# Layer 0 of a four-layer network: inner channels in three parts of 64, with the two token halves side by side on the partitions

## The chip, the cores and the metric

The kernel runs on one core of a Trainium2 chip, in one launch. The metric is the device time of the whole launch in microseconds, the median of several runs. The core has five engines that work side by side, each through its own instructions in order: TensorE (PE, matrix products into PSUM), VectorE (DVE), ScalarE (ACT), GpSimd (POOL) and SyncE (SP), whose queue issues the DMA transfers here. They wait for each other on semaphores.

## The reference

Four layers follow one another. Only the first is changed; the others (a 7x7 depthwise convolution with an MLP, linear attention with a quantised MLP, a Fourier mixer with a quantised MLP) stay as they are.

Layer 0 takes `x` of shape (4, 96, 64, 64) and reads it as 4 sequences of 4096 tokens with 96 channels. Two Mamba blocks follow, each with 192 inner channels and 16 states per inner channel:

```python
h = layernorm(seq) * ln_g + ln_b
xs, z = split(h @ in_w)                      # 192 inner channels each
xc = silu(causal_conv4(xs) + conv_b)
dt, Bm, Cm = split(xc @ xproj_w)             # 6, 16, 16
delta = softplus(dt @ dt_w + dt_b)
h[t] = exp(delta * A) * h[t-1] + delta * Bm * xc      # 192 x 16 recurrences
y = sum over states of h * Cm  +  Dp * xc
seq = seq + (y * silu(z)) @ out_w
```

A pooled projection, a 1x1 fusion, a batch normalisation over all tokens and the residual close the layer. All of it is float32, except for the products that spread B over the partitions (bfloat16, in three parts that together keep the precision).

## The kernel before, in words

**Items.** The 4096 tokens are cut into 4 chunks of 1024. One item is one chunk of one sequence in one Mamba block: 4 x 2 x 4 = 32 items, in an order that lets the carried states of a sequence (`state`) be ready.

**Tiles.** The recurrences of an item are 192 x 16 = 3072 rows of 1024 tokens, so 24 tiles of 128 rows. A tile's rows are 4 states times 32 inner channels. Its name is (half, g, j): which half of 96 inner channels, which four states, which 32 channels of the half. For each tile

- ACT makes the decay `da` as exp(delta * A) from `ddb`, delta repeated over the four states (`exp`, L472);
- DVE multiplies `udb` (delta * xc, repeated) with `rep`, the rows of B spread over the partitions by a matmul into PSUM (`rep`, `scan`, L488); for 8 of the 24 tiles, the pool tiles, POOL makes this product from `brep`, a copy of B by DMA (`times_b`, L478), and ACT writes the decay, `dap`, into PSUM;
- DVE runs the scan (L492);
- POOL multiplies the result with C, repeated (`times_c`, L498, `crep`);
- PE adds up the states with the matrix `sel_r`, 128 rows to 32 (`sum_y`, L515).

`start_y` begins the sum with Dp * xc, `gate` (L526) multiplies it with z on DVE, `project` (L533, L536) adds the output projection to the residual, and `finish` stores it; in the second block it also takes the statistics of the batch normalisation on DVE (L548).

**PSUM.** The tag `xu` has two buffers of [128, 1024]. They go round between `rep`, the product `u` and `dap`. So a `dap` can only be written when DVE has read the last `rep` before it, and a new `rep` only when the scan of the last tile before the pool tile is done.

**First stage.** The work that prepares an item (layer norm, convolution with four taps, `xproj`, `delta`, `z`, the DMA writes of delta and delta * xc to DRAM, and the loads that bring them back repeated) belongs to `first_stage`. It is spread over slots, one per tile of the item before. SiLU and softplus are ACT functions that need a table load before and one after, back to the exponential's tables.

**Order.** For PE, DVE, ACT and POOL the order of instructions is the order in which the program is written (`manual_schedule`): one iteration per tile m issues the scan of m, the `dap` or `rep` of m + 1, the `da` of m + 3, `times_c` of m - 1, `keep_state` of m - 3, a `times_b` by the table `b_slots`, the sums and gates by their place in the item, and last what `first_stage` keeps for this slot. SP's DMA issues follow the same order, and one that waits holds up those behind it.

Before the change the inner channels lie in two halves of 96 partitions, [96, 2, 1024]. The convolution is four units (half, token half) of four taps each. A half has 12 tiles, and its `y` is [96, 1024] in PSUM, in one buffer of two banks. The order of a half's tiles and the pool tiles among them are

```python
half = [(0, 0), (0, 1), (0, 2), (3, 0), (1, 0), (1, 1), (1, 2), (3, 1), (2, 0), (2, 1), (3, 2), (2, 2)]
pool_tiles = (3, 7, 10, 11)
```

Of the kernel before, what the change touches and what calls it, by code (L numbers as in the profile page):

```python
# [32 lines left out]
for _name, _w in (  # L33
    [(f"{k}{i}", w) for i in range(2) for k, w in (("ln_g", 1), ("ln_b", 1), ("conv_w", 8), ("conv_b", 2), ("Dp", 2))]
# [10 lines left out]
for _name, _w in [("A", 48), ("c_b1", 3), ("f2_b1", 3), ("f3_b1", 3), ("id", 48), ("rd", 48), ("rb", 48), ("ib", 48)]:  # L45
    V128[_name] = (_n, _w)
    _n += _w
# [3 lines left out]
class Net:  # L51
# [41 lines left out]
    def layer0(self, dram, scratch):  # L93
        tc, nc, ins = self.tc, self.nc, self.ins
        x_in = ins["x"]
        with ExitStack() as ctx:
# [3 lines left out]
            psum_y = ctx.enter_context(tc.tile_pool(name="l0y", bufs=1, space=PSUM))  # L100
# [12 lines left out]
            w_x = cp.tile([C + 1, 2, 2, 4, C], F32, name="w_x")  # L113
            w_z = cp.tile([C + 1, 2, 2, C], F32, name="w_z")
            sel_b = cp.tile([C, 4, 128], BF16, name="sel_bq")
            part = cp.tile([C, 2, C], BF16, name="partq")
            fo = cp.tile([C, 2, C], F32, name="fo")
            dp = cp.tile([C, 2, 2, C], F32, name="dp")
            sel_r = load(cp, "sel_r", [128, 32])
            xproj = load(cp, "xproj", [C, 2, 2, 3 * 2 * NST + DTR])  # L120
# [3 lines left out]
            out_w = load(cp, "out_w", [C, 2, 2, C])  # L124
# [6 lines left out]
            with tc.tile_pool(name="l0s", bufs=1) as wk:  # L131
# [17 lines left out]
                for i in range(2):  # L149
# [6 lines left out]
                    for k in range(4):  # L156
                        nc.vector.tensor_mul(
                            w_x[:, i, :, k, :],
                            ps[:, :DIN].rearrange("p (h c) -> p h c", h=2),
                            rows[:, i, k].rearrange("p (h c) -> p h c", h=2),  # L160
                        )
                    b = bias[C:, i].rearrange("p (h c) -> p h c", h=2)
                    nc.vector.tensor_add(w_x[C:, i, :, 3, :], w_x[C:, i, :, 3, :], b)
                    nc.vector.tensor_copy(w_z[:, i], ps[:, DIN:].rearrange("p (h c) -> p h c", h=2))
                    for h in range(2):
                        nc.vector.tensor_scalar_mul(dp[:, i, h, :], self.ident[:C, :C], self.v(f"Dp{i}", h))
# [3 lines left out]
                owt = load(wk, "out_wt", [C, DIN])  # L170
                for h in range(2):
                    ps = small(C, C)
                    nc.tensor.matmul(ps, owt[:, h * C : (h + 1) * C], fus[:, 0, :], start=True, stop=True)
                    nc.vector.tensor_copy(fo[:, h, :], ps)
# [273 lines left out]
            def on_pool(m):  # L448
                return m % 12 in pool_tiles
# [992 lines left out]
```

## Time and profile before

| | |
|---|---|
| median of 3 runs | 4220.64 us (4213.79 to 4222.18) |
| the profiled execution | 4226.66 us, its span 4224.9 us |
| mean granted TensorE clock | 0.893 |
| first scan of layer 0 starts | 84.76 us |
| last scan of layer 0 ends | 2714.65 us |
| busy from 200 to 2600 us: PE, DVE, ACT, POOL | 1974, 2301, 1664, 2302 us of 2400 |
| DMA share and rate in that stretch | 0.56, 150 GB/s |

How to read it. The page's second part cuts the span into 40 slices of 105.6 us and gives each engine's busy share in tenths. A line of a group gives the source line, the engine, the operation, output and inputs by the program's names, shapes, the count, the busy time in us, the mean of one in ns, and behind the last bar the idle time of the engine just before these instructions, with what ended most of it. Two matmul records belong to one float32 product here. Matmuls overlap, so the duration of one is longer than the distance to the next. A timeline line gives the start in us, the duration in us and, in brackets, the idle time before it with its releaser.

### The profile page before, as it was taken

How to read it: one execution, taken by the hardware profiler on the slowest of the kernel's cores; microseconds unless marked ns; L12 is line 12 of the kernel's file. 1: busy time of each engine (PE TensorE's matmuls, PEld its weight loads, DVE VectorE, ACT ScalarE, POOL GpSimd, SP SyncE). 2: the span in 40 equal slices, each digit the busy share in tenths (PEclk: the TensorE clock that was granted, in tenths of full speed). 3: DMA queues.
4: the chain of work that ended last, by engine and by line, in shares of the span. 5: the costliest groups of instructions: out<-in, count | busy, mean ns of one | idle time of the engine just before them, and what ended most of it. 6: DMA issues, size and time to landing. Idle time of an engine off the chain costs nothing. (4 is left out here: it accounts for less than half of the span.)

```text
span 4224.9 us, 39882 instructions
## 1 busy us (share of the span) xinstructions
PE 3488.4 (83%) x11934; PEld 1441.2 (34%) x11934; DVE 3216.6 (76%) x2439; ACT 2618.6 (62%) x4194; POOL 3024.1 (72%) x1619
## 2 busy tenths in 40 slices
PE   6788888877887888888778887579999888887987
PEld 2222222222222222222222222177445426555642
DVE  4999999999999999999999999731222583434649
ACT  4776677676666767676676666322555575544547
POOL 2999999999999999999999999711110274333418
PEclk9889988989898898989889888769999998899989
DMA  6556545555655565465456546373000000000111
GB/s 168 142 141 169 146 132 161 156 150 137 168 146 135 154 165 150 133 165 150 137 154 165 149 130 166 84 216 130 0 0 1 1 1 6 23 28 26 46 41 55
DMA packets 168865, 467.62 MB, mean 111 GB/s; under 512 B 51060, under 2 KB 53150, under 8 KB 165568
## 3 DMA queue, kind: packets, MB, share of 16 engines
q1 hardware_dynamic: 168648, 465.07, 41.0%
q8 instruction: 94, 1.54, 0.2%
q14 instruction: 123, 1.01, 0.1%
HBM read 391.40 MB, written 73.50 MB: 110 GB/s over the span
## 5 line engine op out<-in xcount | busy, mean ns | idle before, releaser
L498 POOL TENSOR_TENSOR hs<-hs,crep 128x1024 f32<-128x1024 f32 x768 | 1794.3, 2355 | 108.6 <-DVE hs L492 83.4
L492 DVE TENSOR_TENSOR_SCAN hs<-da,state,u 128x1024 f32<-128x1024 f32 x384 | 901.6, 2348 | 29.3
L515 PE MATMUL y<-hs,sel_r 128*32 128x512 f32 x3072 | 708.4, 674 | 105.4 <-POOL hs L498 105.3
L488 DVE TENSOR_TENSOR u<-udb,rep 128x1024 f32<-128x1024 f32 x512 | 629.1, 1229 | 47.9 <-PE rep L199 17.4
L472 ACT ACTIVATE dap<-ddb,nega 128x1024 f32<-128x1024 f32 x256 | 285.4, 1115 | 520.1 <-DVE u L488 500.3
L478 POOL TENSOR_TENSOR up<-udb,brep 128x1024 f32<-128x1024 f32 x256 | 604.1, 2360 | 3.7 <-DMA brep<-cd 3.7
L472 ACT ACTIVATE da<-ddb,nega 128x1024 f32<-128x1024 f32 x512 | 581.5, 1141 | 1.0
L287 PE MATMUL ps<-n,w_x 97*96 97x512 f32 x1024 | 469.3, 607 | 1.2 <-DVE n L279 1.2
L492 DVE TENSOR_TENSOR_SCAN hs<-dap,state,up 128x1024 f32<-128x1024 f32 x192 | 445.4, 2331 | 0.0
L515 PEld LDWEIGHTS y<-hs,sel_r 128*32 128x32 f32 x3072 | 138.5, 117 | 616.4 <-issue 405.9
L492 DVE TENSOR_TENSOR_SCAN hs<-da,u 128x1024 f32<-128x1024 f32 x128 | 292.9, 2289 | 9.7
L1021 POOL CAST hq<-y 128x512 fp8e5<-128x512 f16 x192 | 118.4, 642 | 222.4 <-DVE y L1020 222.1
L287 PEld LDWEIGHTS ps<-n,w_x 97*96 97x96 f32 x1024 | 165.7, 165 | 274.6 <-issue 254.2
L199 PE MATMUL rep<-r,sel_bq 96*128 96x512 bf16 x384 | 131.3, 427 | 146.6 <-DVE hs L492 146.5
L344 PE MATMUL ps<-dbl,dtw 103*96 103x512 f32 x256 | 179.8, 841 | 52.5 <-ACT r L335 52.5
L293 ACT COPY xc<-ps 96x512 f32<-96x512 f32 x128 | 74.5, 582 | 231.9 <-PE ps L287 231.9
L366 PE MATMUL ps<-n,w_z 97*96 97x512 f32 x256 | 144.2, 691 | 68.4 <-ACT z L372 68.4
L1169 POOL TENSOR_TENSOR av<-av,ec 128x780 f32<-128x780 f32 x32 | 58.8, 1838 | 197.6 <-ACT av L1166 192.2
L815 POOL TENSOR_TENSOR xc<-xc,rs 96x512 f32<-96x512 f32 x32 | 40.4, 1266 | 208.0 <-ACT rs L814 198.2
L389 POOL TENSOR_TENSOR du<-delta,xc 96x1024 f32<-96x1024 f32 x64 | 150.9, 2357 | 27.8 <-ACT delta L359 23.8
L330 PE MATMUL ps<-r,partq 96*96 96x512 bf16 x128 | 49.3, 436 | 124.3 <-ACT r L335 121.4
L492 DVE TENSOR_TENSOR_SCAN hs<-dap,up 128x1024 f32<-128x1024 f32 x64 | 145.6, 2276 | 2.9 <-ACT dap L472 2.1
(255 smaller groups left out, 6305.4 us busy)
## 6 DMA issues: line engine op xcount, KB each, us to landing
ddb<-dd SPq DMA_DIRECT2D x768, 128.0 KB, 3.8
udb<-ud SPq DMA_DIRECT2D x768, 128.0 KB, 3.2
crep<-cd SPq DMA_DIRECT2D x512, 128.0 KB, 4.2
brep<-cd SPq DMA_DIRECT2D x256, 128.0 KB, 4.3
dd<-delta SPq DMA_DIRECT2D x64, 384.0 KB, 4.0
ud<-du SPq DMA_DIRECT2D x64, 384.0 KB, 5.4
band<-in_band SPq DMA_DIRECT2D x24, 1024.0 KB, 4.8
gt<-in_idft SPq DMA_DIRECT2D x64, 256.0 KB, 2.9
```

What stands on the lines that cost most here:

```text
L199: nc.tensor.matmul(ps[:, at], w, rhs[:, at_in], start=start, stop=stop, **kw)
L287: nc.tensor.matmul(ps, w_x[:, i, o, k], n[:, at.start + k : at.stop + k], start=k == 0, stop=k == 3)
L344: nc.tensor.matmul(ps, dtw[:, i, h * C : (h + 1) * C], dbl[:, at], start=True, stop=True)
L366: nc.tensor.matmul(ps, w_z[:, i, o], rhs, start=True, stop=True)
L389: nc.gpsimd.tensor_mul(u, m["delta"][:, h], m["xc"][:, h])
L472: nc.scalar.activation(da, made[k]["dd", h, j], AF.Exp, scale=nega[:, col : col + 1])
L478: nc.gpsimd.tensor_mul(u, made[k]["ud", h, j], made[k]["brep", g])
L488: nc.vector.tensor_mul(u, made[k]["ud", h, j], x)
L492: nc.vector.tensor_tensor_scan(hs[:, 1:], made[k].pop(("da", t)), u, 0.0 if s == 0 else st, ALU.mult, ALU.add)
L498: nc.gpsimd.tensor_mul(hs[:, :T], hs[:, 1:], made[k]["crep", order[t][1]])
L515: nc.tensor.matmul(made[k]["y"][32 * j : 32 * j + 32, at], sel_r, made[k]["hs", t][:, at], start=False, stop=True, skip_group_check=True,)
L1021: nc.gpsimd.tensor_copy(q[:, m, :], y2, saturate=False)
```

## The change

The 192 inner channels become three parts of 64. On the partitions lie the 64 channels of a part for the first 512 tokens and, below them, the same 64 channels for the second 512: [128, 3, 512] in place of [96, 2, 1024] for `xc`, `delta` and `z`. `spread` makes such a part with pairs of 64-column matmuls, one into partitions 0 to 63 and one into 64 to 127 of a PSUM bank; `join` reads it with 64-row matmuls, one per token half, into two banks. Part p has 8 tiles (two groups of 32 channels, four groups of states), of which the pool tiles are 2, 5, 7, 10, 13, 15, 18 and 21 of the item's 24. `y` becomes [128, 512], one bank, with two buffers, and the sums are taken two tiles at a time, one gate per part. Nine `rep` an item take the place of six. The slots of the first stage, of the loads and of `times_b` move; the output projection goes from slot 4 of the next item to slot 15; `crep` gets five buffers for four and one of the two `brep` gets two. The weights are laid out to suit, on the host.

The diff, without the tables of constants, the set-up of the weights and their layout on the host:

```diff
-            psum_y = ctx.enter_context(tc.tile_pool(name="l0y", bufs=1, space=PSUM))
+            psum_y = ctx.enter_context(tc.tile_pool(name="l0y", bufs=2, space=PSUM))
...
+            both = [(at, slice(64 * q, 64 * q + 64)) for q, at in enumerate(halves)]
+
+            def spread(ws, rhs, p):
+                ps = tile_ps(128)
+                for k, (w, shift) in enumerate(ws):
+                    for at, rows in both:
+                        nc.tensor.matmul(
+                            ps[rows],
+                            w[:, 64 * p : 64 * p + 64],
+                            rhs[:, at.start + shift : at.stop + shift],
+                            start=k == 0,
+                            stop=k == len(ws) - 1,
+                            skip_group_check=True,
+                        )
+                return ps
+
+            def join(pss, w, x, start=True):
+                for p in range(3):
+                    for ps, (at, rows) in zip(pss, both):
+                        nc.tensor.matmul(ps, w[rows, p], x[rows, p], start=start and p == 0, stop=p == 2)
...
-                units = [(o, at) for o in range(2) for at in halves]
-                for t, unit in enumerate(units):
-                    at_slot(t - 1)(lambda unit=unit: conv(*unit))
...
-                    at_slot(t)(lambda unit=unit: evict(*unit))
+                def parts_of(name, ws, rhs, slots, bufs):
+                    def into(p, ps):
+                        if p == 0:
+                            m[name] = wk.tile([128, 3, MB], F32, name=name, tag=name, bufs=bufs)
+                        nc.scalar.copy(m[name][:, p], ps)
+
+                    for p, (t, out) in enumerate(slots):
+                        at_slot(t)(lambda p=p: m.update({(name, p): spread(ws, rhs, p)}))
+                        at_slot(out)(lambda p=p: into(p, m[name, p]))
+
+                parts_of("xc", [(w_x[:, i, k], k) for k in range(4)], n, ((-1, 0), (0, 1), (2, 3)), 2)
...
-                @at_slot(6)
+                @at_slot(5)
                 def _():
                     m["ps"] = [tile_ps(128), tile_ps(128)]
...
+                    join([ps[:nb] for ps in m["ps"]], xproj[:, :, i], m["xc"])
...
-                    at_slot(8 + 2 * r)(lambda r=r: less(r))
-                    at_slot(9 + 2 * r)(lambda r=r: next_part(r))
...
-                at_slot(12)(lambda: dt(0))
-                at_slot(13)(lambda: dt_out(0))
-                at_slot(13)(lambda: dt(1))
-                at_slot(14)(lambda: dt_out(1))
-
-                @at_slot(15)
+                    at_slot(7 + 2 * r)(lambda r=r: less(r))
+                    at_slot(8 + 2 * r)(lambda r=r: next_part(r))
+
+                parts_of("delta", [(dtw[:, i], 0)], dbl, ((10, 11), (10, 11), (11, 12)), 1)
+
+                @at_slot(12)
                 def _():
                     nc.scalar.activation(m["delta"], m["delta"], AF.Softplus)
                     exp_set()
...
-                at_slot(15)(lambda: z_in(0))
-                at_slot(16)(lambda: z_out(0))
-                at_slot(16)(lambda: z_in(1))
-                at_slot(17)(lambda: z_out(1))
+                parts_of("z", [(w_z[:, i], 3)], n, ((16, 17), (16, 17), (17, 18)), 2)
...
+                @at_slot(13)
                 def _():
+                    m["dd"] = dram.tile([DIN, T], F32, name="dd", tag="dd", bufs=2)
+                    for at, rows in both:
+                        nc.sync.dma_start(m["dd"].rearrange("(p c) t -> c p t", p=3)[:, :, at], m["delta"][rows])
...
-                at_slot(17)(lambda: du(0))
-                at_slot(22)(lambda: du(1))
+                at_slot(14)(lambda: du(0, 1))
+                at_slot(20)(lambda: du(1, 2))
...
+                for p in range(3):
+                    for j in range(2):
+                        at_slot((16, 24, 32)[p] + j)(lambda p=p, j=j: load_d(m, "dd", p, j))
+                        at_slot((18, 26, 34)[p] + j)(lambda p=p, j=j: load_d(m, "ud", p, j))
+                for g, t in ((0, 10), (1, 21), (3, 23), (2, 25)):
+                    at_slot(t)(lambda g=g: load_c(m, g))
+                at_slot(12)(lambda: load_b(m, 3))
+                at_slot(15)(lambda: load_b(m, 2))
...
-            pool_tiles = (3, 7, 10, 11)
+            eight = [(0, 0), (0, 1), (3, 0), (1, 1), (1, 0), (3, 1), (2, 0), (2, 1)]
+            order = [(p, g, j) for p in range(3) for g, j in eight]
+            pool_tiles = (2, 5, 7, 10, 13, 15, 18, 21)
+            group_starts = (0, 3, 6, 8, 11, 14, 16, 19, 22)
...
+            def start_y(k, p):
+                y = made[k]["y", p] = psum_y.tile([128, MB], F32, name="y", tag="y")
+                nc.tensor.matmul(y, dp[:, items[k][2], p], made[k]["xc"][:, p], start=True, stop=True)
+
+            def sum_y(k, t0):
+                for q, at in enumerate(halves):
+                    for t in (t0, t0 + 1):
+                        p, g, j = order[t]
+                        row = 64 * q + 32 * j
+                        nc.tensor.matmul(
+                            made[k]["y", p][row : row + 32],
+                            sel_r,
+                            made[k]["hs", t][:, at],
...
+            def gate(k, p):
+                z = made[k]["z"][:, p]
+                nc.vector.tensor_mul(z, made[k]["y", p], z)
...
+                pss = made[k]["out"] = [tile_ps(), tile_ps()]
+                for at, ps in zip(halves, pss):
+                    w = fus[:, 0] if i else self.ident[:C, :C]
+                    nc.tensor.matmul(ps, w, made[k]["x"][:, at], start=True, stop=False)
+                join(pss, fo if i else out_w, made[k]["z"], start=False)
...
-            b_slots = {0: 3, 4: 7, 7: 10, 9: 11, 12: 15, 15: 19, 18: 22, 20: 23}
+            b_slots = {2: 5, 4: 7, 7: 10, 9: 13, 12: 15, 15: 18, 18: 21, 23: NTL + 2}
...
-
-                        if t == 2 and m >= 0:
-                            xu_next = rep(m + 2)
-                        elif on_pool(m) and not on_pool(m + 1):
-                            xu = xu_next if t == 3 and m >= 0 else rep(m + 1)
+                        elif (t + 1) % NTL in group_starts:
+                            xu = rep(m + 1)
...
+                        at = m - NTL * k0
+                        for p in range(3):
+                            if at == 8 * p + 3:
+                                start_y(k0, p)
+
+                            if at - 8 * p in (4, 6, 8, 10):
+                                sum_y(k0, at - 4)
+                            if at == 8 * p + 11:
+                                gate(k0, p)
+                        if at == 34:
+                            made[k0]["x"] = load_x(*items[k0])
+                        if at == 39:
+                            project(k0)
+                        if at == 40:
+                            finish(k0)
```

## The prediction

> **What bounds the kernel now.** I began with the page: its busy shares by slice and its groups.
>
> ```profile
> PE   6788888877887888888778887579999888887987
> ...
> DVE  4999999999999999999999999731222583434649
> ...
> POOL 2999999999999999999999999711110274333418
> ...
> L498 POOL TENSOR_TENSOR hs<-hs,crep 128x1024 f32<-128x1024 f32 x768 | 1794.3, 2355 | 108.6 <-DVE hs L492 83.4
> L492 DVE TENSOR_TENSOR_SCAN hs<-da,state,u 128x1024 f32<-128x1024 f32 x384 | 901.6, 2348 | 29.3
> ```
>
> DVE and POOL are both at 90% or more through slices 2 to 25, which is layer 0 and nothing else. So layer 0 lasts as long as the slower of the two. POOL's idle time ends on a DVE scan (83.4 us of 108.6): POOL waits for DVE. Next, what DVE waits for: its groups from 100 to 3000 us.
>
> ```profile
> L488 DVE TENSOR_TENSOR u<-udb,rep 128x1024 f32<-128x1024 f32 x509 | 625.4, 1229 | 45.6 <-PE rep L199 17.4 <-DVE hs L492 0.5
> ...
> L526 DVE TENSOR_TENSOR z<-y,z 96x1024 f32<-96x1024 f32 x64 | 76.5, 1195 | 6.9 <-PE y L515 6.9
> L279 DVE TENSOR_TENSOR n<-n,ps 96x512 f32<-96x512 f32 x60 | 37.7, 667 | 0.0
> L548 DVE BATCH_NORM_STATS2 stats<-o 96x6 f32<-96x512 f32 x32 | 20.6, 681 | 24.6 <-ACT o L547 24.6
> ```
>
> The named waits are small: 17.4 us for the matmul `rep`, 24.6 us for the output `o`. The rest is instruction spacing. Adding the gaps before DVE's instructions by place in the item (timeline) puts the first on tile 8 (1.2 us in items without statistics), the second on tile 6 (1.3 to 2.2 us in items with them). From first scan (84.76 us) to last (2714.65) 32 items take 82.2 us each.
>
> ScalarE has slack but strict order: its timeline before one pool tile.
>
> ```profile
> 1548.71 1.12 ACT L472 ACTIVATE dap<-ddb,nega 128x1024 f32<-128x1024 f32 x1 [2.32 <-DVE u L488]
> ...
> 1551.08 1.28 ACT L399 ACT_TABLE_LOAD   x1
> 1552.37 1.91 ACT L399 ACTIVATE z<-z 96x2048 f32<-96x2048 f32 x1
> 1554.29 1.28 ACT L202 ACT_TABLE_LOAD   x1
> ...
> 1558.44 1.12 ACT L472 ACTIVATE dap<-ddb,nega 128x1024 f32<-128x1024 f32 x1 [0.74 <-DVE u L488]
> ```
>
> A `dap` may start only when DVE has read the last `rep` of its group, and must end before that tile's scan. Here a SiLU with two table loads fits between two `dap`, with 0.74 us over. Starts in this timeline give ACT's pitches: exponential 1.05, state copy 0.1, PSUM copy 0.5 us.
>
> [...] The trace has 32-wide column tiles only: twelve L515 matmuls start at 1507.67 and take 1.92 us; three start within 0.02 us, each round 0.43 us after the last. The first L315 after them starts 0.52 us after their last round[...]. No run shows 64-wide tiles. [...] L287 has 607 ns (0.43 us pitch), while matmuls that come after waits are slower (L344 841, L267 939 ns; 0.86 us pitch).
>
> **The change part by part.** Sums are for 32 items, against the profiled execution (4224.9 us span in a 4226.66 us run).
>
> 1. Scans (24 an item), products `u` (16), pool tiles (8) and `times_b` (8) keep number and shape. Nothing.
>
> 2. Gate. 64 x 1195 ns become 96 of 128x512; nearest row L279, 667 ns. 76.5 - 64.0 = 12.5 us. Consecutive DVE instructions without a wait overlap by some 0.08 us at either side, so 32 more hide 5 us. **-17 us**, on the path.
>
> 3. `du`: 64 x 2357 ns become 32 of half the length and 32 of the full one, 32 x (1.2 + 2.36) = 114 us, 37 less on POOL. POOL waits for DVE already: **0**. If DVE were no longer slowest, it would count.
>
> 4. ACT: `xc`, `delta`, `z` copies fall from 12 to 9 an item (-1.7 us), three 2048-long functions (1.91) become 1536 (about 1.48, scaled): -1.3. ACT idles for DVE: **0** by itself; it shortens part 7.
>
> 5. PE. The sums take 20 rounds of 0.43 us per half-item before (2+2, 4+4, 4+4), 40 an item; with four row groups at once 12 x 2 = 24: -6.9 us. Convolution: 32 passes become 24 pairs, -3.4; z, delta, xproj, output projection and Dp about -0.8 each, -4; three more `rep` (6 to 9), +1.3. PE is not the bound, so this is worth only the waits it ends. `rep` for tile 8: the projection into `dbl` now goes two tiles earlier and ends about 2 us before `rep` may start; -17. `o`: the output projection moves to slot 15, starts once `rep(16)` is out, 3.2 us after the product of tile 14; 4 x 0.43 for x, 6 x 0.43 joined, `o` at 7.9 to 9.0. DVE ends scan 16 at 8.45 and has the first statistics at 8.6: of 24.6, 2 stay. **-40 us** together. If row tiles don't pair, +2.6 us in 16 items gives 40 back.
>
> 6. Loads. The same 72 tile loads an item; `dd` still two writes, `ud` four for two, of 2 KB rows. SP's order: slot 20's `ud` waits for `du` at about 71 us of an item, and `crep` 1, `crep` 3 and part 1's `ddb` queue behind it: 4 + 12 issues x 0.42 us + 4.2 to land, about 82. Their first user is tile 2's `times_c` at 93. `times_b` is three or four tiles ahead, by my count of POOL's queue finished at least 4.7 us early. **0**.
>
> 7. The new wait. ACT between pool tiles: SiLU of `xc` (slot 3) now has `dap(5)` one slot behind it; before, three. From the end of product 1: scan 1 ends at 2.44, which frees the buffer for `rep(3)`; PE sends it, then the sums of tiles 22 and 23 (two rounds), then the third convolution part, eight rounds from 3.95, ending at 7.55. Copy, load, SiLU, load: 0.6 + 1.29 + 1.48 + 1.29 = 4.7; `dap(5)` from 12.3 to 13.4, scan at 13.5. DVE would have reached it at 12.8 (scan, pool scan 2.25, product and scan 3.75, gate 0.7, product and scan 3.75, overlaps off). **0.7 us late**. PE has idled 4 us before the first part, so half its rounds may be at half clock; `rep(3)` then starts 0.9 later: 1.6. I take 1.1 an item, **+35 us** (22 to 51). The same count for the softplus (slot 12, `dap(15)`) leaves 0.2 us to spare, for z's SiLU (slot 19, `dap(21)`) it is 0.1 late, 0.6 cold: **+5 us** (0 to 20). What is late next is POOL, which has 2 us an item to spare.
>
> 8. Ends. Before the first scan PE runs the convolution back to back (32.3 to 46 us), 24 pairs for 32 passes, -3.4; SiLU, softplus, z -1.3; projections and copies -3: **-8 us**. After the last scan two tiles' sums remain instead of five, in two rounds, at half clock: **-4**.
>
> Sum: -17 - 40 + 35 + 5 - 12 = **-29**; 4224.9 becomes 4196. The three runs' median is 6 us under the profiled run, so I forecast **4190**.
>
> **Rivals.**
>
> A. The moved SiLU and a colder PE eat all of it. Part 7 at its high ends, 51 + 20, and 6 us for `rep` behind a cold copy of z: -17 - 40 + 77 - 12 = +8: 4233 profiled, 4227 against the median. For: PE's work falls by about 13 us an item, so more idle windows. Against: L287 averages 607 ns today, and a gap of 2.7 us before L366 left it fast in 21 of 24 cases.
>
> B. **Slower: 64-wide matmuls don't pair.** Then each convolution part is 16 passes, 6.9 us, in slots 23, 0 and 2. From the end of product 23 PE needs 0.5 + 6.9 + 1.0 + 6.9 = 15.3 before `rep(3)`, wanted done by 12.1: 3.8 us late. The third part ends 23.8, `dap(5)` 29.7, wanted 24.1: 5.7 more. 32 x 9.5 = 304, so 4225 + 304 - 57 - 12 = 4460. It decides once a part takes over about 4.5 us. [...]
>
> C. No new wait: part 7 is nothing, because the copy comes earlier. -69: 4150.
>
> D. POOL becomes the bound. Its busy time was 80.5 us an item and loses 1.2: 79.3, some 2 us under DVE's 81.6. At 79.3 the end would be C's, 4150, no sooner; it cannot make the kernel slower.
>
> Between A and B lies a case with SiLU waits of 3 us an item (convolution at half clock throughout): about 4260.
>
> **How the numbers follow.** Forecast as worked (4165 to 4209 on the median's scale) 0.50; C 0.07; A, within or just above 0.2%, 0.18; 3 us waits 0.14; B 0.09; the remaining 0.02 is loads that come late. The range from 4145 to 4270 leaves out B and the ends. Of this, 0.2% (8 us) being what a measurement can tell from no change: faster 0.57, same 0.13, slower 0.30. As cases of both signs hold chance, the likeliest one's own range is 4165 to 4209.
>
> **What would show it.** Right: the period from first to last scan falls to about 81.6 us an item; DVE's waits for `rep` and `o` shrink to a few us; a new wait of some 0.7 to 1.6 us stands before the scan of tile 5, released by ACT `dap`, and little anywhere else; convolution matmuls start in pairs; POOL still waits for DVE. The forecast is wrong if pairs start 0.43 us apart (B), if tile 5's scan waits over 2 us, if `rep` for tile 3 or 19 comes late, or if scans wait for `up`, which would mean POOL or the loads.

## The result, and the profile after

| | before | after |
|---|---|---|
| median of the runs taken together | 4217.22 us (4211.04 to 4222.18, 4 runs) | 4347.61 us (4337.53 to 4361.05, 4 runs) |
| ratio | | 1.031, 95% interval 1.028 to 1.034 |
| profiled execution, its span | 4226.66, 4224.9 us | 4361.05, 4359.3 us |
| mean granted TensorE clock | 0.893 | 0.827 |
| first scan starts, last scan ends | 84.76, 2714.65 us | 83.41, 2843.25 us |
| from first to last scan | 2629.9 us | 2759.8 us |
| an item (a 32nd of that) | 82.2 us | 86.2 us |

The change makes the kernel 3.1% slower. 4190 had been forecast, and the time lies beyond the upper end of the range, 4270. Of the 134.4 us between the two spans, 129.9 lie between the first scan and the last. The rest of the span is 1595.0 us before and 1599.5 after. The granted clock is the share of TensorE's full clock that it is given. In the clock records of both traces it is 1.0 or 0.5 at any moment, called full and half clock below, so a mean of 0.893 says that 21% of the span was at half clock, and 0.827 that 35% was. A round is one matmul record, or several side by side, and its pitch is the distance from its start to the start of the next.

The page of the changed kernel, its slices and groups:

```profile
PE   6677677767677677676777676587999987878887
...
DVE  5999988899989898989899989941221393443639
...
POOL 2999988899889898998889899811111064433418
PEclk8778777878777778777877787668999998998989
...
L481 POOL TENSOR_TENSOR hs<-hs,crep 128x1024 f32<-128x1024 f32 x768 | 1798.1, 2356 | 222.9 <-DVE hs L475 193.0
...
L195 PE MATMUL rep<-r,sel_bq 96*128 96x512 bf16 x576 | 234.8, 500 | 723.3 <-DVE hs L475 513.8
...
L205 PE MATMUL ps<-n,w_x 97*64 97x512 f32 x1536 | 438.7, 721 | 2.9 <-DVE n L299 2.8
```

The same lines of the kernel before, as far as they have not been shown:

```profile
PEclk9889988989898898989889888769999998899989
...
L287 PE MATMUL ps<-n,w_x 97*96 97x512 f32 x1024 | 469.3, 607 | 1.2 <-DVE n L279 1.2
...
L199 PE MATMUL rep<-r,sel_bq 96*128 96x512 bf16 x384 | 131.3, 427 | 146.6 <-DVE hs L492 146.5
```

Against the page of before, the slices of DVE and POOL have fallen from nines to eights and nines, and POOL's idle time still ends on DVE's scans (193.0 of 222.9 us): DVE is the slower of the two and has begun to wait. The granted clock, mostly 8 and 9 tenths before, is mostly 7 and 8. The matmul `rep` has become slower, 500 ns for 427, and the convolution matmul too, 721 for 607.

DVE's groups from 100 to 3000 us, the last column being the idle time before them with its releasers:

```profile
L471 DVE TENSOR_TENSOR u<-udb,rep 128x1024 f32<-128x1024 f32 x508 | 622.8, 1226 | 76.1 <-PE rep L195 50.2 <-DVE hs L475 0.9
L475 DVE TENSOR_TENSOR_SCAN hs<-dap,state,up 128x1024 f32<-128x1024 f32 x192 | 448.0, 2333 | 81.1 <-ACT dap L455 51.9 <-ACT state L488 27.2 <-POOL hs L481 1.7
...
L475 DVE TENSOR_TENSOR_SCAN hs<-dap,up 128x1024 f32<-128x1024 f32 x63 | 143.4, 2277 | 28.2 <-ACT dap L455 14.6 <-ACT state L488 13.6
L511 DVE TENSOR_TENSOR z<-y,z 128x512 f32<-128x512 f32 x96 | 64.0, 667 | 4.5 <-PE y L500 4.5
...
L530 DVE BATCH_NORM_STATS2 stats<-o 96x6 f32<-96x512 f32 x32 | 20.5, 681 | 53.2 <-ACT o L529 53.2
```

The gate is as forecast: 64.0 us. The waits are not. `rep` went from 17.4 to 50.2 us, `o` from 24.6 to 53.2, and the scans of pool tiles, with next to no wait before, now have 81.1 + 28.2. Part of these is put down to the small copy of `state`; ACT issues it right behind `dap`, and it ends 0.1 us after it, so both labels mean the same wait.

One item shows how it comes about. PE's timeline around its first scan (850.47 us):

```profile
846.79 1.03 PE L195 MATMUL rep<-r,sel_bq 96*128 96x512 bf16 x2 [6.93 <-DVE u L471]
847.75 6.67 PE L205 MATMUL ps<-n,w_x 97*64 97x512 f32 x16
854.35 1.07 PE L500 MATMUL y<-hs,sel_r 128*32 128x512 f32 x8
855.35 3.65 PE L205 MATMUL ps<-n,w_x 97*64 97x512 f32 x16
858.94 0.60 PE L195 MATMUL rep<-r,sel_bq 96*128 96x512 bf16 x2
859.47 1.06 PE L500 MATMUL y<-hs,sel_r 128*32 128x512 f32 x8
860.47 3.65 PE L205 MATMUL ps<-n,w_x 97*64 97x512 f32 x16
```

After 6.93 us without work PE starts `rep` and the first part of the convolution, and that part takes 6.67 us. The same 16 records take 3.65 us twice further on. So it ran at half clock nearly to its end: pitches of 0.86 us in seven of eight rounds, where the others have 0.43. Two rounds of sums and the second part follow; `rep` for tile 3 starts at 858.94, the third part ends at 864.12. ACT's timeline from there:

```profile
864.17 0.59 ACT L309 COPY xc<-ps 128x512 f32<-128x512 f32 x1 [3.31 <-PE ps L205]
864.77 1.28 ACT L320 ACT_TABLE_LOAD   x1
866.07 1.49 ACT L320 ACTIVATE xc<-xc 128x1536 f32<-128x1536 f32 x1
867.57 1.28 ACT L222 ACT_TABLE_LOAD   x1
868.87 1.12 ACT L455 ACTIVATE dap<-ddb,nega 128x1024 f32<-128x1024 f32 x1
```

The chain is the one that part 7 of the prediction counted: copy, table load, SiLU, table load, `dap` for tile 5, ending at 869.99. DVE in the same stretch:

```profile
859.58 1.23 DVE L471 TENSOR_TENSOR u<-udb,rep 128x1024 f32<-128x1024 f32 x1 [0.80 <-PE rep L195]
...
865.01 2.35 DVE L475 TENSOR_TENSOR_SCAN hs<-da,state,u 128x1024 f32<-128x1024 f32 x1
870.09 2.35 DVE L475 TENSOR_TENSOR_SCAN hs<-dap,state,up 128x1024 f32<-128x1024 f32 x1 [2.73 <-ACT state L488]
```

DVE waits 0.80 us for the `rep` of tile 3 and 2.73 us before the scan of tile 5. Three of the prediction's own signs of being wrong are there: over 2 us before tile 5, and a late `rep` at tiles 3 and 19 (the table below).

For all 32 items I added up DVE's gaps of more than 0.2 us between the first and the last scan, by the tile that they stand ahead of, from the trace of each kernel (the runs below are in it too). The values are us over the whole stretch; small entries are left out, the sum holds all:

| kernel | tile 3 `rep` | 5 `dap` | 8 `rep` | 16 `rep` | statistics | 18 `dap` | 19 `rep` | 21 `dap` | sum | first to last scan |
|---|---|---|---|---|---|---|---|---|---|---|
| before | | | 17.4 | | 20.5 | | | | 42.5 | 2629.9 |
| after | 19.8 | 84.8 | | | 45.4 | 10.6 | 30.8 | 13.5 | 205.8 | 2759.8 |
| e1_warm | | 35.6 | 22.2 | 12.9 | 14.4 | | 17.8 | 8.4 | 118.1 | 2671.8 |
| e2_warm22 | | 35.9 | | | 50.2 | 18.8 | 31.3 | 13.8 | 157.0 | 2713.7 |
| e3_silu | 17.6 | | | | 41.0 | 7.7 | 32.6 | 13.5 | 113.2 | 2663.6 |
| e4_proj | 19.9 | 81.8 | | | | | 38.4 | 6.1 | 147.0 | 2699.4 |
| v1_silu_proj | 16.6 | | | 5.0 | | | 38.3 | 5.9 | 67.1 | 2615.5 |
| v2_silu_proj_warm | | | 9.9 | 4.9 | | | 37.9 | 6.3 | 64.8 | 2613.9 |
| v3_z_late | | | 7.7 | 10.5 | | | | 78.1 | 102.7 | 2654.5 |
| v4_silus | 20.9 | | | | | | | 13.5 | 39.4 | 2588.5 |
| v5_silus_warm | | | 12.3 | 1.3 | | | | 14.0 | 32.3 | 2581.9 |
| b1_light | | | 9.1 | | 13.2 | | | | 26.4 | 2615.0 |

With this the difference adds up, from the first scan's start to the last one's: DVE's busy time -12.7 us (2549.1 to 2536.5), gaps over 0.2 us +163.3, small gaps less overlaps -20.7 (35.9 to 15.2), together +129.9.

### The profile page after: what moved, and what is told of

Read it like the earlier page. It is cut to its first block, busy times and chain, and to the rows that moved or that the text cites. A ratio compares the mean times of both kernels' runs of the same rounds, so it can differ in the third digit from the quotient of the medians.

```text
span 4359.3 us, 42251 instructions
## 1 busy us (share of the span) xinstructions
PE 3285.0 (75%) x13088; PEld 1297.7 (30%) x13088; DVE 3191.1 (73%) x2474; ACT 2522.3 (58%) x4098; POOL 2995.3 (69%) x1619
## 5 line engine op out<-in xcount | busy, mean ns | idle before, releaser
L481 POOL TENSOR_TENSOR hs<-hs,crep 128x1024 f32<-128x1024 f32 x768 | 1798.1, 2356 | 222.9 <-DVE hs L475 193.0
L195 PE MATMUL rep<-r,sel_bq 96*128 96x512 bf16 x576 | 234.8, 500 | 723.3 <-DVE hs L475 513.8
L471 DVE TENSOR_TENSOR u<-udb,rep 128x1024 f32<-128x1024 f32 x512 | 627.7, 1226 | 76.2 <-PE rep L195 50.2
L475 DVE TENSOR_TENSOR_SCAN hs<-dap,state,up 128x1024 f32<-128x1024 f32 x192 | 448.0, 2333 | 81.1 <-ACT dap L455 51.9
L500 PE MATMUL y<-hs,sel_r 128*32 128x512 f32 x3072 | 490.6, 712 | 6.0 <-POOL hs L481 6.0
L205 PE MATMUL ps<-n,w_x 97*64 97x512 f32 x1536 | 438.7, 721 | 2.9 <-DVE n L299 2.8
L195 PEld LDWEIGHTS <-sel_bq 96*128 96x128 bf16 x576 | 47.3, 102 | 972.6 <-issue 530.7
L309 ACT COPY xc<-ps 128x512 f32<-128x512 f32 x96 | 56.3, 587 | 432.0 <-PE ps L205 432.0
L205 PEld LDWEIGHTS ps<-n,w_x 97*64 97x64 f32 x1536 | 121.8, 163 | 308.4 <-issue 286.0
L205 PE MATMUL ps<-n,w_z 97*64 97x512 f32 x384 | 110.9, 688 | 66.3 <-ACT z L309 66.3
L500 PEld LDWEIGHTS y<-hs,sel_r 128*32 128x32 f32 x3072 | 65.1, 115 | 298.2 <-issue 229.2
L1140 ACT ACTIVATE av<-xr_ps,vec 128x65 f32<-128x65 f32 x384 | 117.0, 425 | 46.2 <-PE xr_ps L1128 46.2
L373 POOL TENSOR_TENSOR du<-delta,xc 128x512 f32<-128x512 f32 x64 | 116.2, 1816 | 36.1 <-ACT delta L357 31.2
```

Source lines behind the costliest of these rows:

```text
L195: nc.tensor.matmul(ps[:, at], w, rhs[:, at_in], start=start, stop=stop, **kw)
L205: nc.tensor.matmul(ps[rows], w[:, 64 * p : 64 * p + 64], rhs[:, at.start + shift : at.stop + shift], start=k == 0, stop=k == len(ws) - 1, ...
L373: nc.gpsimd.tensor_mul(u, m["delta"][:, of], m["xc"][:, of])
L471: nc.vector.tensor_mul(u, made[k]["ud", h, j], x)
L475: nc.vector.tensor_tensor_scan(hs[:, 1:], made[k].pop(("da", t)), u, 0.0 if s == 0 else st, ALU.mult, ALU.add)
L481: nc.gpsimd.tensor_mul(hs[:, :T], hs[:, 1:], made[k]["crep", order[t][1]])
```

## The experiments

**The theory after the result.** PE has less to do, so it stands idle for 4 to 7 us ahead of some `rep`, and what it does then runs at half clock for several us: the `rep` itself and whatever stands between it and the next function of ACT. The rival: the new places alone (the third part one slot ahead of the SiLU, the projection in slot 15, z ahead of the `rep` of tile 19) are to blame, whatever PE's clock. Four kernels were compared first, each the changed kernel with one edit.

**e1_warm: more work for PE where it stands idle.** Matmuls with a weight of zeros, which add nothing to `y`:

```diff
+            def warm(k, p, count):
+                for _ in range(count):
+                    nc.tensor.matmul(made[k]["y", p], zw, ..., start=False, stop=True, ...)
...
+            WARM = {6: (0, 4), 9: (0, 4), 14: (1, 4), 22: (2, 7)}      # slot: (part, count)
...
+                    if 0 <= m < last and t in WARM:
+                        warm(k, *WARM[t])
```

> The changed kernel, with 128-wide matmuls of zero weights that add 0 to the open y, put where PE stands idle: four in slots 6, 9 and 14 and seven in slot 22 (0.86 us each at full clock). Theory 1, half clock: PE, made lighter, idles for more than 4 us before the rep of tiles 8, 11, 16 and 24 and then works at half clock for some 6 us, so that the first convolution part and the projection come late. Then this run has full clock there: the wait at tile 5 falls from 2.7 to about 0.7 us an item, that of the statistics from 3.0 to about 0, that of tile 19 to 0, and the time goes to about 4180 us. Theory 2, order alone (the place of the SiLU, and rep before the convolution in PE's queue): more work on PE changes nothing or delays rep further, 4350 us or more.

Measured: 4262.03 us (4255.13 to 4265.5), 1.0087 of before (1.0063 to 1.0111), where the changed kernel has 1.031. PE's work went up and the kernel became 85 us faster. The busy times from 200 to 2600 us, first of the changed kernel, then of this one, the columns being the window's length, then PE, PE's weight loads, DVE, ACT and POOL with their instructions, then the granted clock, the DMA share and GB/s:

```profile
200.00:2600.00 2400.00, 1699.15 (x6460) 418.24 (x6460) 2172.05 (x1277) 1502.71 (x2211) 2168.72 (x995) 0.79 0.58 144
```

```profile
200.00:2600.00 2400.00, 2065.62 (x7776) 609.14 (x7778) 2249.85 (x1323) 1558.80 (x2273) 2247.56 (x1029) 0.92 0.61 149
```

PE goes from 1699 to 2066 us busy, the clock from 0.79 to 0.92, and DVE's busy time, which in a window of fixed length shows the kernel's pace, from 2172 to 2250. DVE's groups:

```profile
L473 DVE TENSOR_TENSOR u<-udb,rep 128x1024 f32<-128x1024 f32 x508 | 622.8, 1226 | 83.9 <-PE rep L197 50.5 <-DMA crep<-cd 3.4 <-DMA ud<-du 2.0
L477 DVE TENSOR_TENSOR_SCAN hs<-dap,state,up 128x1024 f32<-128x1024 f32 x192 | 447.8, 2332 | 30.3 <-ACT state L490 17.7 <-ACT dap L457 12.4
...
L477 DVE TENSOR_TENSOR_SCAN hs<-dap,up 128x1024 f32<-128x1024 f32 x63 | 143.4, 2276 | 14.8 <-ACT state L490 9.6 <-ACT dap L457 5.0
...
L543 DVE BATCH_NORM_STATS2 stats<-o 96x6 f32<-96x512 f32 x32 | 20.5, 681 | 19.1 <-ACT o L542 19.1
```

The waits before pool tiles have fallen from 109.3 to 45.1 us, the one for statistics from 53.2 to 19.1. This speaks for the half clock. But 4180 or so had been expected with it, and 118 us of gaps are left. 35 of them are of the added work's own making: the matmuls of slots 6 and 14 stand ahead of the `rep` of tiles 8 and 16 and make those late (22.2 and 12.9). Of the other 83, 76 stand at tiles 5, 19, 21 and the statistics, with PE at full clock (warm) most of the time, at a mean clock of 0.92: about that much the places cost. So both theories hold a share.

**e2_warm22: the seven matmuls of slot 22 alone.**

```diff
+            WARM = {22: (2, 7)}
```

> As the run before, but only the seven matmuls of slot 22, ahead of the first convolution part. Theory 1: the waits at tiles 3 and 5 shrink by some 2.7 us an item together, the statistics still wait 3 us, time about 4262 us. Theory 2: 4350 us or more.

Measured: 4304.61 us (4295.05 to 4308.9), 1.0186 of before (1.0161 to 1.0211). PE's timeline around the first scan of the same item (835.54 us):

```profile
824.82 6.28 PE L513 MATMUL y<-w_x,zw 97*128 97x512 f32 x14
831.86 0.61 PE L197 MATMUL rep<-r,sel_bq 96*128 96x512 bf16 x2 [0.77 <-DVE u L473]
832.40 3.65 PE L207 MATMUL ps<-n,w_x 97*64 97x512 f32 x16
835.98 1.07 PE L502 MATMUL y<-hs,sel_r 128*32 128x512 f32 x8
836.98 3.65 PE L207 MATMUL ps<-n,w_x 97*64 97x512 f32 x16
```

The added matmuls end 0.77 us ahead of `rep`, and the first part takes 3.65 us for 6.67. Nothing else was moved, and the waits before tile 3 and tile 5 went from 104.6 us to 35.9; the others stayed or grew by up to 8, and 4.7 came before tile 0. That the half clock of the first part causes two thirds of these two waits is thereby shown. What is left before tile 5, 35.9 us or 1.1 an item, is the cost of the place. The 4262 us that theory 1 gave was missed by 43: the two waits shrank by 2.1 us an item and not by 2.7, and part of it came back in the other places.

**e3_silu: the SiLU of `xc` one slot later**, behind the `dap` of tile 5:

```diff
-                @at_slot(3)
+                @at_slot(4)
                 def _():
                     nc.scalar.activation(m["xc"], m["xc"], AF.Silu)
```

> The changed kernel with one edit: the SiLU of xc stands in slot 4, so that dap of tile 5 goes ahead of it on ACT, whatever PE's clock is. Both theories: the wait at tile 5 (2.7 us an item) goes, the one for rep of tile 3 (0.65 us) stays, time about 4262 us. A third theory, that ACT has too much between pool tiles 2 and 7 wherever the SiLU stands: the wait moves to tile 7 or to rep of tile 8, and the time stays above 4330 us.

Measured: 4256.54 us (4250.49 to 4260.98), 1.0073 of before (1.0045 to 1.0101). DVE's groups:

```profile
L475 DVE TENSOR_TENSOR_SCAN hs<-dap,state,up 128x1024 f32<-128x1024 f32 x192 | 447.4, 2330 | 13.8 <-ACT dap L455 13.5
...
L475 DVE TENSOR_TENSOR_SCAN hs<-dap,up 128x1024 f32<-128x1024 f32 x63 | 143.3, 2274 | 7.8 <-ACT dap L455 7.6
...
L530 DVE BATCH_NORM_STATS2 stats<-o 96x6 f32<-96x512 f32 x32 | 20.5, 681 | 49.5 <-ACT o L529 49.5
```

The wait at tile 5 is gone (84.8 us in the table), the others stand as they were, and the time fell by 91 us. So SiLU ahead of `dap` is what makes it wait, and the SiLU has the room to go later.

**e4_proj: the output projection one slot earlier**, with its load of x:

```diff
-                        if at == 34:
+                        if at == 32:
                             made[k0]["x"] = load_x(*items[k0])
-                        if at == 39:
+                        if at == 38:
                             project(k0)
```

> The changed kernel with one edit: the output projection one slot earlier (38 for 39, its x loaded at 32 for 34), ahead of rep of tile 16 and in PE's idle time. The statistics stop waiting (3 us in 16 items, 48 us); PE no longer idles before rep of tile 16. Theory 1: time about 4300 us, with z and tile 19 a little earlier as well, so down to 4275 us. Theory 2: rep of tile 16 comes late behind the projection, up to 2 us in every item, 4350 us or more.

Measured: 4292.2 us (4283.64 to 4301.97), 1.0161 of before (1.0133 to 1.0188), 55 us under the changed kernel. DVE's groups:

```profile
L475 DVE TENSOR_TENSOR_SCAN hs<-dap,state,up 128x1024 f32<-128x1024 f32 x192 | 447.8, 2332 | 65.4 <-ACT state L488 42.5 <-ACT dap L455 22.0
...
L530 DVE BATCH_NORM_STATS2 stats<-o 96x6 f32<-96x512 f32 x32 | 20.1, 669 | 7.9 <-ACT o L529 7.9
```

What the projection looks like where it stands behind the `rep` of tile 16, first in the changed kernel, then in e1_warm:

```profile
902.30 1.01 PE L195 MATMUL rep<-r,sel_bq 96*128 96x512 bf16 x2 [4.37 <-DVE hs L475]
903.11 3.62 PE L518 MATMUL ps<-x,ident 96*96 96x512 f32 x4
```

```profile
888.20 1.88 PE L531 MATMUL ps<-x,ident 96*96 96x512 f32 x4
```

In e4_proj the statistics' wait is gone between first and last scan (7.9 us lie after the last), with the one at tile 18; `rep` for tile 19 waits 7.6 us more. With the clock as it was, the place alone mends it. As e1_warm took two thirds of it away with the place as it was (45.4 to 14.4 us), it takes both to make it: a projection put behind the `rep` of tile 16, and a PE that has idled 4.4 us ahead of that `rep`, so that the x matmuls run at a pitch of 0.86.

**The edits together.** v1_silu_proj joins e3_silu and e4_proj. v2_silu_proj_warm adds the seven matmuls of e2_warm22. v3_z_late moves the third part of z behind the `rep` of tile 19 as well:

```diff
-                parts_of("z", [(w_z[:, i], 3)], n, ((16, 17), (16, 17), (17, 18)), 2)
+                parts_of("z", [(w_z[:, i], 3)], n, ((16, 17), (16, 17), (18, 19)), 2)
```

> The changed kernel with the SiLU of xc in slot 4 and the output projection at 38. Theory 1 (the waits stand side by side, each is worth its own size): the SiLU run left 1.36 us an item for the statistics, and the projection run took that away and added 0.18 before tile 19. So 32 x 1.2 = 38 us under the SiLU run: 4218, 82.1 us an item. Theory 2 (each wait that goes is followed by the next, which PE at half clock makes): no better than the SiLU run, 4245 to 4260.

> The same with seven added zero-weight matmuls in slot 22. Theory 1: the wait for the rep of tile 3 (0.59 us an item) goes too, tile 19 keeps 1.0 to 1.2: 4199, 81.5 us an item. Theory 2: the seven matmuls only move the wait to tile 19 or 21: 4218 or more.

> The kernel with SiLU in slot 4, projection at 38 and seven added matmuls, and the third part of z one slot later (18, its copy in 19), so that the rep of tile 19 goes out ahead of it. Theory 1: the wait at tile 19 (1.0 to 1.2 us an item) goes, the SiLU of z comes up to 1 us later and tile 21 waits 0.4 to 1.0: 4167 to 4199. Theory 2 (the late rep of tile 19 is the half clock of the matmul itself, not z in front of it): the wait stays within 0.2 us of what it was, so 4199 to 4220.

Measured: v1_silu_proj 4204.12 us (4198.56 to 4210.62), 0.996 of before (0.994 to 0.998). That is 14 us better than theory 1 had it. 8 of them are the kernel before, which had 4217.66 beside these runs and 4225.63 beside the first four; for the rest, the `dap` of tiles 18 and 21 wait less too (21.2 us in e3_silu, 5.9 here). Waits mended one by one add up. v2_silu_proj_warm 4197.35 us (4192.68 to 4202.73), 0.994 (0.992 to 0.996): the number expected, but not by the way expected. The wait at tile 3 (16.6 us) goes, 9.9 come at tile 8 and 3.7 at tile 0, and the ranges of the two kernels' runs overlap: warming PE there is worth at most a few us once the SiLU is out of the way.

v3_z_late fell short: 4237.34 us (4229.14 to 4244.74), 1.0039 (1.0031 to 1.0047). DVE's groups:

```profile
L473 DVE TENSOR_TENSOR u<-udb,rep 128x1024 f32<-128x1024 f32 x508 | 622.8, 1226 | 53.2 <-PE rep L197 20.6 <-DMA ud<-du 1.8 <-DVE hs L477 1.4
L477 DVE TENSOR_TENSOR_SCAN hs<-dap,state,up 128x1024 f32<-128x1024 f32 x192 | 447.2, 2329 | 56.7 <-ACT dap L457 56.7
```

Its first half came as theory 1 had it: with z out of its way the `rep` of tile 19 no longer waits (37.9 us to none). But the copy of z now reaches ACT in slot 19, ahead of z's SiLU and its two table loads, and behind those stand the copies of the next item's centred x and the `dap` of tile 21: 78.1 us of wait where 13 to 32 had been expected. It is the same fault as the one of tile 5, made once more, and PE is cold (at half clock) there too: it idles 4.56 us ahead of the `rep` of tile 19 in the item looked at, and the four records of z behind it take 1.98 us, where e1_warm has 1.08.

**b1_light: the kernel before with less for PE.** The sums over the second token half are left out, 20 of 40 rounds an item; that half of `y` lacks those terms.

```diff
-                            if at in (4, 5):
+                            if at == 4:
                                 sum_y(k0, [o + 0, o + 1, o + 2], halves[at - 4])
-                            if at in (8, 9):
+                            if at == 8:
...
-                                for at_half in halves:
+                                for at_half in halves[:1]:
```

> The kernel before, with the sums over the states of the second token half left out (20 of 40 rounds of 0.43 us an item, 8.6 us of PE's work; that half of the output lacks those terms). Nothing else is moved. Theory 1 (PE with less to do goes to half clock ahead of its reps and convolutions): granted clock below 0.87, waits for rep at tile 8 and for dap grow, slower than before by 10 to 80 us. Theory 2 (a lighter PE only ends waits; the changed kernel's waits come from the new places alone): 4195 to 4226, the clock as before.

Measured: 4210.2 us (4201.67 to 4215.1), 0.9971 of before (0.9959 to 0.9984). Theory 1 was right about the clock and wrong about the waits; theory 2 was right about the time and wrong about the clock. The busy times from 200 to 2600 us, of before, then of this kernel:

```profile
200.00:2600.00 2400.00, 1974.46 (x5701) 573.25 (x5703) 2301.38 (x1311) 1664.03 (x2385) 2301.65 (x1042) 0.89 0.56 150
```

```profile
200.00:2600.00 2400.00, 1816.55 (x4333) 537.43 (x4333) 2317.09 (x1320) 1675.70 (x2397) 2315.20 (x1049) 0.81 0.56 151
```

```profile
L488 DVE TENSOR_TENSOR u<-udb,rep 128x1024 f32<-128x1024 f32 x508 | 624.1, 1228 | 38.0 <-PE rep L199 9.1 <-DVE hs L492 0.5 <-DMA udb<-ud 0.2
L492 DVE TENSOR_TENSOR_SCAN hs<-dap,state,up 128x1024 f32<-128x1024 f32 x192 | 445.5, 2331 | 0.1
...
L548 DVE BATCH_NORM_STATS2 stats<-o 96x6 f32<-96x512 f32 x32 | 20.6, 681 | 18.3 <-ACT o L547 18.3
```

The clock fell from 0.89 to 0.81, nearly the 0.79 of the changed kernel, `rep` and convolution became slower (491 and 671 ns for 426 and 607), and still no wait grew; `rep` and the statistics wait less than before. So a clock nearly as low as the changed kernel's doesn't slow every schedule. What half clock alone would cost this one stays open, as the rounds left out also free PE's queue ahead of some `rep`. In the kernel before, the next `dap` stands three slots behind the SiLU of `xc`, not one, and no scan came to wait behind a slow matmul. That a cold PE costs time only where the order leaves no room for it fits this run and e3_silu (91 us faster than the changed kernel, at a clock of 0.83 from 200 to 2600 us); the first four runs alone did not tell it.

**v4_silus and v5_silus_warm: room for z's SiLU too.** To v3_z_late's late z comes the SiLU of z in slot 22, behind the `dap` of tile 21 and behind the functions of the layer norm; v4_silus has no added matmuls, v5_silus_warm the seven of slot 22.

```diff
-                @at_slot(19)
+                @at_slot(22)
                 def _():
                     nc.scalar.activation(m["z"], m["z"], AF.Silu)
```

> The changed kernel with the SiLU of xc in slot 4, the projection at 38, the third part of z in slot 18 (copy in 19), and the SiLU of z in slot 22 for 19, behind the dap of tile 21. No matmuls are added, PE stays as cold as it was. Theory 1 (a late matmul or SiLU costs only where a rep or dap is queued right behind it): the waits at 19 (1.19 us an item) and 21 (0.18) go and none comes, 4204 - 44 = 4160 (4150 to 4175), about 80.4 us an item. Theory 2 (PE at half clock gives another late rep for each that is mended): a new wait of 0.5 to 1 us before tile 0, 3 or 22, 4175 to 4204.

> The same with the seven added zero-weight matmuls in slot 22. Theory 1: the wait before tile 3 (0.55 us an item) goes, and 0.3 comes before tile 8, as with the seven added before: 4152 to 4160. Theory 2: as before, 4175 to 4200.

Measured: v4_silus 4181.51 us (4177.4 to 4183.25), 0.9892 of before (0.9873 to 0.9911); v5_silus_warm 4165.18 us (4155.34 to 4168.22), 0.9851 (0.9832 to 0.987). Both beat both kernels; the kernel before had 4224.92 beside them. The `rep` of tile 19 no longer waits, but v4_silus is 6 us above theory 1's range, and its time lies in theory 2's: `dap` of tile 21 waits 13.5 us, where the 5.9 of v1_silu_proj were to go, and tile 3 has 20.9 for 16.6. The new wait that theory 2 names is there, at tile 22, but with 2.9 us in all where 16 to 32 had been said. v5_silus_warm is 5 us over theory 1's range, with tile 8 where tile 3 was. Of its 16 us under v4_silus only 6.6 lie between first and last scan; 9.6 lie behind the last one, where the two programs are the same. That end takes from 1497 to 1516 us in the twelve traces, of one execution each. DVE's groups in v5_silus_warm:

```profile
L473 DVE TENSOR_TENSOR u<-udb,rep 128x1024 f32<-128x1024 f32 x507 | 621.6, 1226 | 45.5 <-PE rep L197 15.8 <-DVE hs L477 1.4 <-DMA crep<-cd 0.4
L477 DVE TENSOR_TENSOR_SCAN hs<-dap,state,up 128x1024 f32<-128x1024 f32 x192 | 447.1, 2329 | 10.8 <-ACT dap L457 10.8
...
L477 DVE TENSOR_TENSOR_SCAN hs<-dap,up 128x1024 f32<-128x1024 f32 x62 | 140.8, 2272 | 3.3 <-ACT dap L457 3.2
...
L543 DVE BATCH_NORM_STATS2 stats<-o 96x6 f32<-96x512 f32 x32 | 20.1, 668 | 4.7 <-ACT o L542 4.7
```

Against the changed kernel, `rep` waits 15.8 us for 50.2, the pool tiles 14.1 for 109.3, the statistics 4.7 for 53.2. Its clock from 200 to 2600 us is 0.86, still under the 0.89 of the kernel before. In both kernels the first scan starts some 4 us earlier than in the changed kernel (79.25 and 78.62 us). Most of that arises ahead of z's SiLU: the twelve dt matmul records of the first item take 2.84 us in both, at full clock, where they take 5.39 in the changed kernel, and the softplus starts at 60.67 and 60.41 us for 63.97. Why the clock was full there in these two traces is not shown; in v1_silu_proj, v2_silu_proj_warm and v3_z_late it was not.

## Why the prediction was wrong

**Right.** What bounds the kernel: POOL still waits for DVE. Part 1: the scans' busy time is 1787.8 before and 1788.4 us after. Part 2: the gates take 64.0 us as worked out. Part 3, `du` at nothing: right, for the reason given. Part 4's ACT items are shorter, 1.49 us for a SiLU. Part 6: none of DVE's waits between first and last scan is put down to a load; POOL has some 24 us of such waits, inside its idle time. The pairing of 64-wide matmuls, my estimate, which no run had shown (only 32-wide sums were seen side by side, three within 0.02 us): the whole warm part of eight rounds takes 3.65 us, so rival B falls, and with it its 4460. Rival D did not arise, as DVE fell behind POOL, not the other way round. The place of the new wait, its chain and the five lengths in it (0.6 + 1.29 + 1.48 + 1.29 and `dap`) are as in part 7.

**Part 7, the step that failed most: a size.** It took 1.1 us an item before tile 5, 35 us in all. It is 84.8. The 1.1 is what the place costs with a warm PE: e1_warm and e2_warm22 have 35.6 and 35.9 us, where the count for a warm PE had given 0.7 an item, so that hitting 1.1 there is chance. I had the first part at half clock for at most half its rounds, 0.9 us of delay for the `rep` of tile 3, and took the middle of that. That 4 us without work would bring half clock, and for so many rounds, was my estimate: of the two slow matmuls named in the prediction, L344 (841 ns) has 0.2 us of idle time ahead of a record (52.5 in all), L267 (939 ns) less than 0.03, and I had not read from the trace of before how long a wait brings half clock, nor how long that lasts. Measured, seven of eight rounds are at half clock, 3.0 us more for the part, and in the item shown that `rep` starts 2.4 us after the scan that frees its buffer has ended (856.54 us). The idle time ahead of it was taken as 4 us; it is 6.93. The 19.8 us at tile 3 come from the same error, and part 7 did not count them at all: `rep` for tile 3 stands behind this part.

**Part 5, a wait that came back.** Its -40 us came as said: the 17.4 us of tile 8 and the 20.5 us of tile 6 are gone. But "of 24.6, 2 stay" was worked out with PE warm, `o` at 7.9 to 9.0 us after product 14. The projection stands behind a gap of 4.4 us with its x matmuls at half clock, and the statistics wait 45.4 us, more than what the move removed. The added matmuls cut it to 14.4, the earlier slot to nothing.

**Parts 7 and 5, what was not followed further.** Behind the late projection come z and, behind z, the `rep` of tile 19: 30.8 us, and `dap` of tile 18, 10.6. I had `rep` behind a cold copy of z at 6 us, in rival A only. z's SiLU at tile 21 cost 13.5 us, inside its 0 to 20. The softplus's tile 15 has no wait, as said.

**Part 8.** The first scan is 1.4 us earlier, not 8: PE pauses between the steps ahead of it, the `xproj` and dt matmuls ran mostly at half clock there (twelve records each, 4.52 and 5.39 us), and the softplus came as late as before. After the last scan 1510.2 became 1516.0 us where 4 less had been expected. The last gate does start 2.4 us sooner after the last scan, but the output projection behind it runs mostly at half clock, 7.8 us for 5.4, and the last aggregate of the statistics ends up 0.7 us later. The rest lies in the later layers and is no more than the scatter of that end between the traces.

**The sum** was -29. The terms as measured: -12.7 busy, -37.9 for the two old waits, +204.9 for six new ones (+40 had been taken), -3.7 for the other gaps over 0.2 us, -20.7 for small gaps and overlaps (-5 had been taken), +4.5 outside: +134.4.

**The rivals.** A named the right mechanism, moved SiLUs and a colder PE that eat the gain, and priced it at 77 us; it is 205. The case of 3 us at tile 5 (0.14 of the chance) has that wait nearly right at 2.65, and stopped there. Both were wrong in the main for one reason: the colder PE was priced at one place and not at every `rep` and `dap` behind a gap. Of the 205 us some 76 are left in e1_warm at these places, with PE mostly warm, so that the places themselves were priced too low too. The argument against A, that a gap of 2.7 us had left a matmul fast in 21 of 24 cases, was read from one line of the kernel before, where gaps are shorter. It does not hold as it stands: the 2.7 us run from start to start, the idle time is 2.1, and the first matmul behind it is fast in 18 of these 24. The same trace also spoke for A: of 21 gaps of 2.4 to 2.9 us ahead of the sums (L515), 20 were followed by half clock. I had lightened PE by 13 us an item and never asked where those 13 us would stand as idle time. They stand in single pieces of 3 to 7 us, 111 of 123 of them right ahead of a `rep` and the others ahead of z.

## What to carry to other kernels

When a change makes a waiting engine lighter, ask where its freed time will stand: in the changed kernel each of the 123 idle pieces of PE of 3 us or more was followed by half clock, with full clock back a median of 6.4 us after the first matmul behind it, and if a `rep`, or an ACT function with a release behind it, is queued right there, work saved becomes time lost. Where the order has room a cold PE need not cost much (b1_light, and v4_silus, whose gaps come to 39.4 us at a mean clock of 0.855), so look at what is issued behind each gap, not at the mean clock. An ACT function with two table loads took 4.1 us in a row here (1.28 + 1.49 + 1.28 us and the steps between them); it goes right behind the last release that another engine needs, not right ahead of the next.

## What was unexpected of the hardware

- In the changed kernel's trace from 200 to 2600 us, PE's gaps (from the modelled end of one matmul to the start of the next, those over 0.3 us) fall into two kinds. After 122 of the 123 gaps of 3 us or more TensorE was at half clock for most of the next 2 us, in 120 of them for all of it; after the other one it was from 1.06 us on. Of 111 gaps under 2 us 24 were followed by half clock, and 22 of these lay in a stretch at half clock that had begun before the gap. From the first matmul behind a gap of 3 us or more, full clock was back after a median of 6.4 us (3.5 to 15.3, the longest with a further gap in between).
- In the clock record of the same trace and window, of 99 stretches at half clock one lasted 3.4 us, 44 lasted 6.8, 29 10.2 and 25 13.7 or 17.1.
- The length of a gap does not decide alone. In the kernel before, 20 of 21 gaps of 2.4 to 2.9 us ahead of the sums were followed by half clock, and after 11 of 16 gaps of 3.5 to 4 us the clock stayed full for at least the next 1 us. The 13 gaps of 2.4 to 2.9 us ahead of a `rep` left it full over the next 1 us.
- More work made the kernel faster: 19 added matmuls an item, 85 us less (e1_warm against the changed kernel). And 20 rounds less an item made the kernel before faster by 0.3% only, at a clock of 0.81.
- Two 64-column matmuls side by side take the time of one: eight rounds of pairs, 16 float32 records, take 3.65 us at a pitch of 0.43, the pitch that single convolution matmuls have in the kernel before.
